# First routing of a two-pass tree network: the upper node weights loaded alone, the lower ones turned beside the token groups

## The chip, the cores and the metric

The kernel runs on one core of a Trainium2 chip. The metric is the device time of one execution in microseconds; of several executions the median is given. Engines are called as in the profile: PE (matrix products and transposes), PEld (its weight loads), DVE, ACT, POOL and SP. DMAs are issued by SP, ACT and POOL; SPq, ACTq and POOLq stand for the issuing of those queues.

## The reference, cut to what matters

```python
x = x + 0.5 * ffn(layernorm(x))        # x: (4, 1024, 256)
x = x + attention(layernorm(x))
x = x + 0.5 * ffn(layernorm(x))        # the same weights again

def fff(x, nw, nb, w1, b1, w2, b2, act):      # a tree of 255 nodes and 256 leaves
    node = 0
    for _ in range(8):
        logit = x . nw[node] + nb[node]
        node = 2 * node + 1 + (logit > 0)
    leaf = node - 255
    return act(x @ w1[leaf] + b1[leaf]) @ w2[leaf] + b2[leaf]

def ffn(x):
    xn = (x - mean) / sqrt(std + 1e-5)
    q, k, v = fff(xn, q_*), fff(xn, k_*), fff(xn, v_*)
    y = xn + softmax(q k^T / 16) v
    return y + fff(y, f_*)
```

Each of the four trees (q, k, v, f) has node weights `nw` (255 x 256), node thresholds `nb`, and for each leaf a 256x16 matrix, a 16x256 matrix and two biases.

## The kernel before, in words

The 4096 tokens are 32 tiles of 128 rows (NT = 32), taken in eight groups of four tiles (GT = 4). A tree is cut at depth 5: the 31 upper nodes decide to which of 32 blocks a token belongs, and the lower nodes are evaluated inside a block, together with the leaves. So an ffn begins with a **routing**: for each group the four tiles are normalized, turned by PE, multiplied with the upper nodes of q, k and v (`top`), compared with the thresholds (`thr`), and from the bits comes a one-hot block number `oh`; POOL adds them up in `acc`. From `oh` and `acc` the **placement** works out where each token goes (`slot`) and which token stands where (`inv`). With `inv_q` POOL gathers rows of 128 tokens of one block (`gathered`, L826), and the **leaves** of q, then k, then v run on them. Scores, softmax and the tree f follow, then the attention, then a second ffn.

What happens before the first gather is what this change touches:

- `hold_rows()` and two calls of `load_x` load the first two groups of x by SP; the other six groups are asked for inside `ffn`, behind the nodes.
- Nodes, L185 to L210. For each tree SP loads all 255 node rows in two tiles `nw` of 128 rows, PE turns them (L196), DVE copies them to `nwT` (L205), and ACT issues the load of the thresholds (L200) and the store of the lower nodes to the DRAM tensor `below` (L206). At the end the thresholds are negated (L209) and `top` is copied out of `nwT` (L210).
- L212 to L278 make small constant tables with some 45 short DVE instructions. The tables `anc` and `rights` are needed for `oh`.
- `split_b2` splits the second biases of all trees in three bfloat16 parts on POOL (casts L320, subtractions L328) and stores them in `b2i` (L323). Its loads `b_rest` are issued by ACT (L310).
- `ffn`: with `first` set, SP gets the loads of the first leaf weights (`load_raw`, 1 MB each, L718), the second leaf weights of q (`load_second`, 4 MB, named w_q<-in_q_w in the profile, L701) and the split biases (`load_b2`, L998), which wait for `b2i`.
- `routes(hp, (0, 1, 2), *hot, norms)` runs the eight groups. `norms(k)` takes means and variances of the group (L340, L341), the two square roots and reciprocals (`both_norms`, L348 to L357, and L1137), normalizes on ACT (L1165) and stores the normalized rows for the gathers (`keep_rows`, by ACT, L376). From k = 4 on it also advances `build`, which turns the leaf weights of q (L772, copies L775 and L777); the first step of `build` loads `sub` from `below` (L757) and copies it on POOL (L760).
- After `routes` come `load_b1` (48 small loads by SP, L733 and L738, with POOL work at L743 to L751) and the rest of the placement of q, whose last product is `inv_q` (L624).

The order of the instructions on each engine is not that of the program text: outside the sections marked `in_order()`, a planner places each instruction by program order and by its own estimate of when its inputs are there. On the chip each engine then runs its list strictly in order, so an instruction that waits holds everything behind it. `tc.keep_in_program_order` fixes the place of single instructions relative to others marked so.

Of the kernel before, what the change touches and what calls it, by code (L numbers as in the profile page):

```python
# [16 lines left out]
F32 = mybir.dt.float32  # L17
# [8 lines left out]
P = 128  # L26
# [4 lines left out]
KC = E // P  # L31
# [47 lines left out]
def macaron_kernel(ctx: ExitStack, tc: tile.TileContext, a: dict, out: bass.AP):  # L79
# [32 lines left out]
    def sm(shape):  # L112
        return bank("sm", shape)
# [71 lines left out]
    b2i = [dram.tile([3, B2P], BF16, name=f"b2i_{nm}") for nm in FFFS]  # L185

    with tc.tile_pool(name="nodes", bufs=2) as np_, banks(0, 8):
        nwT = np_.tile([P, KC, len(FFFS), 2 * P], F32, name="nwT", bufs=1)
        nc.vector.memset(thr, 0.0)
        for f, nm in enumerate(FFFS):  # L190
            pt = [sm([P, 2 * P]) for _ in range(KC)]
            for lo in (0, NODES - P):
                nw = np_.tile([P, E], F32, name="nw", bufs=8)
                nc.sync.dma_start(nw, a[f"{nm}_nw"][lo : lo + P, :])
                for c in range(KC):
                    nc.tensor.transpose(  # L196
                        pt[c][:, lo : lo + P], nw[:, c * P : (c + 1) * P], ident
                    )
            lo = f % 3 * NBLK
            nc.scalar.dma_start(  # L200
                thr[lo : lo + NBLK - 1, f // 3 : f // 3 + 1],
                a[f"{nm}_nb"][: NBLK - 1].unsqueeze(1),
            )
            for c in range(KC):
                nc.vector.tensor_copy(nwT[:, c, f, :NODES], pt[c][:, :NODES])  # L205
            nc.scalar.dma_start(  # L206
                below[f].rearrange("p (c n) -> p c n", c=KC), nwT[:, :, f, NBLK - 1 : NODES]
            )
        nc.vector.tensor_scalar_mul(thr, thr, -1.0)  # L209
        nc.vector.tensor_copy(top, nwT[:, :, :, :NBLK])  # L210

        nc.vector.memset(mod32, 0.0)  # L212
        t1 = np_.tile([P, 1], F32, name="t1", bufs=1)
# [86 lines left out]
    nc.vector.tensor_scalar_add(zero[:, E:], pid, float(NTOK))  # L300
    nc.gpsimd.dma_start(rows_x[NTOK:], zero[:, :E])

    def split_b2(pool):

        n = NBLK // B2G * E
        rest = pool.tile([P, n], F32, name="b2_rest")
        none = pool.tile([P, 3 * B2P // P // 2], BF16, name="b2_none")
        nc.gpsimd.memset(none, 0.0)
        for f, nm in enumerate(FFFS):
            nc.scalar.dma_start(  # L310
                rest[f * NBLK : (f + 1) * NBLK].rearrange("p (q c) -> p q c", c=E),
                a[f"{nm}_b2"].rearrange("(q p) c -> p q c", p=NBLK),
            )
            nc.gpsimd.dma_start(
                b2i[f].rearrange("s n -> (s n)").rearrange("(p i c) -> p i c", p=P, i=2),
                bc(none, 1, 2),
            )
        for s in range(3):
            part = pool.tile([P, n], BF16, name=f"b2_part{s}", tag="b2_part", bufs=2)
            nc.gpsimd.tensor_copy(part, rest)  # L320
            for f in range(len(FFFS)):
                rows = b2i[f][s].rearrange("(r n) -> r n", r=B2G)[:, : EPB * B2W]
                nc.gpsimd.dma_start(  # L323
                    rows.rearrange("r (e w) -> r e w", e=EPB)[:, :, :n],
                    part[f * NBLK : (f + 1) * NBLK],
                )
            if s < 2:
                nc.gpsimd.tensor_sub(rest, rest, part)  # L328
# [46 lines left out]
    def keep_rows(queue, lo, hi):  # L375
        queue.dma_start(  # L376
            rows_x[lo * P : hi * P].rearrange("(i p) e -> p i e", p=P), xn[:, lo:hi, :E]
        )
# [45 lines left out]
    def routes(pool, fs, oh, acc, before):  # L424


        n = NT // GT
        live = {}
        before(0)
        for k in range(n + 2):  # L430
            for j in (k - 1, k - 2, k):
                if 0 <= j < n:
                    if j == k:
                        live[k] = route(pool, fs, k * GT, oh, acc)
                    next(live[j], None)
            if k + 1 < n:
                before(k + 1)
# [551 lines left out]
    def load_b2(queue, pool, f):  # L989

        return fill_b2(
            queue, pool.tile([B2R, B2W], BF16, name=f"b2s_{FFFS[f]}", tag="b2s"), f
        )

    def fill_b2(queue, b2s, f):

        for s in range(3):
            queue.dma_start(  # L998
                b2s[s * NBLK : (s + 1) * NBLK],
                b2i[f][s, : NBLK * B2W].rearrange("(p w) -> p w", p=NBLK),  # L1000
            )
        return b2s

    def fetch(pool, f, t, slot, bufs=3, tag=None, to=None):
# [50 lines left out]
    def ffn(first: bool, last: bool):  # L1055

        def drain(*gens):
            for g in gens:
                for _ in g:
                    pass  # L1060
# [6 lines left out]
        with ExitStack() as es:  # L1067
# [31 lines left out]
            with ExitStack() as ws, banks(0, 8):  # L1099
# [8 lines left out]
                with ExitStack() as hs, ExitStack() as rs:  # L1108
# [11 lines left out]
                    with ExitStack() as rt:  # L1120
# [26 lines left out]
                            build = iter(())  # L1147
                            load_kept(nc.sync, 0, w1)
                        w2 = load_second(nc.sync, wp, 0)
                        b2s = load_b2(nc.sync, wp, 0)  # L1150
                        low, rest = placing(pq, 0, ahead=True)

                        def norms(k):
                            lo = k * GT
                            ts_ = range(lo, lo + GT)
                            if first:
                                for t in ts_:
                                    rows_moments(hp, mom[:, t, :], x_of(t))
                                both(lo, GT)
                            elif lo in (0, NT - TPB):  # L1160
                                n = TPB if lo else NT - TPB
                                both(lo, n, f"_{n}")
                            for t in ts_:
                                if first or t % 2:
                                    nc.scalar.activation(  # L1165
                                        x_of(t),
                                        x_of(t),
                                        AF.Identity,
                                        bias=shift[t],
                                        scale=scale[t],  # L1170
                                    )
                                else:
                                    nc.vector.tensor_scalar(
                                        x_of(t),
                                        x_of(t),
                                        mom[:, t, 0:1],
                                        scale[t],
                                        ALU.subtract,
                                        ALU.mult,
                                    )  # L1180
                            keep_rows(nc.scalar, lo, lo + GT)
                            if k in (4, 6):
                                drain(low(k // 2 - 2))
                            if k >= 4:
                                drain(islice(build, 2))

                        routes(hp, (0, 1, 2), *hot, norms)
                        drain(low(2))
                        if first:
                            for f in range(len(FFFS)):  # L1190
# [778 lines left out]
```

## Time and profile before

| what | value |
|---|---|
| runs | 2414.78, 2422.02, 2427.72 us; median 2422.02 us |
| the profiled execution | 2422.62 us, span 2420.8 us |
| PE busy | 2164.4 us (89%) |
| DVE, ACT, POOL busy | 1428.0 us (59%), 1073.0 us (44%), 850.1 us (35%) |
| mean granted clock of PE | 0.953 |
| from 0 to 116 us: PE, DVE, ACT, POOL busy | 57.1, 76.0, 36.5, 53.4 us |
| from 116 to 240 us: PE busy | 107.5 us |
| moved by DMA in all | 305.26 MB |

In a timeline line the first number is the start in microseconds from the start of the span, the second the time it took (or, for several merged instructions, the time they span), then engine, line, operation, the tile written and the tiles read, and the count. In brackets stands how long the engine had been idle before, and what ended that. In a line of waits the three numbers are the total, how often, and the longest one.

### The profile page before, as it was taken

What the parts mean: (1) busy time and instruction counts of PE and PEld (TensorE: products, weight loads), DVE (VectorE), ACT (ScalarE), POOL (GpSimd) and SP (SyncE); (2) the same over time, 40 slices, a digit from 0 to 9 for tenths busy, and PEclk for the clock granted to TensorE, in tenths of its full rate; (3) what the DMA queues carried; (4) which work ended last, traced back from release to release, by engine and by line L of the source; (5) the groups of instructions that cost most, each with busy time, mean ns of one, the idle gap of its engine ahead of it and who ended that gap; (6) DMA issues with size and microseconds to landing.
All of it is one profiled execution on the core that took longest, in us unless ns stands there. A gap on an engine that the chain in (4) does not pass through costs nothing. (4 is left out here: it accounts for less than half of the span.)

```text
span 2420.8 us, 43067 instructions
## 1 busy us (share of the span) xinstructions
PE 2164.4 (89%) x13969; PEld 1383.2 (57%) x13971; DVE 1428.0 (59%) x4804; ACT 1073.0 (44%) x2875; POOL 850.1 (35%) x1078
## 2 busy tenths in 40 slices
PE   4598898999997889999999999997597998999968
PEld 2377787676666744433444344334486785666657
DVE  6677655333447766666667667754775653334656
ACT  2355556233323324555555555555264663232234
POOL 4455466342524521100100110001454673245546
PEclk8799999999998979999999999999799999999989
DMA  9787776344544400000000000006568666342375
GB/s 317 243 273 227 251 227 204 103 138 122 163 146 149 150 1 1 1 1 1 1 8 12 1 3 19 17 1 228 194 187 261 170 175 206 96 140 90 125 222 170
DMA packets 201714, 305.26 MB, mean 126 GB/s; under 512 B 26185, under 2 KB 172698, under 8 KB 196864
## 3 DMA queue, kind: packets, MB, share of 16 engines
q1 hardware_dynamic: 106432, 114.60, 14.7%
q0 software_dynamic: 37264, 96.33, 14.4%
q10 hardware_dynamic: 57776, 91.32, 11.2%
q8 instruction: 125, 2.05, 0.4%
q14 instruction: 117, 0.96, 0.1%
HBM read 185.37 MB, written 121.49 MB: 127 GB/s over the span
## 5 line engine op out<-in xcount | busy, mean ns | idle before, releaser
L1719 DVE TENSOR_REDUCE mxh<-big 128x1 f32<-128x512 f32 (+3 forms) x768 | 392.7, 551 | 195.8 <-PE big L1711 194.0
L1755 ACT ACTIVATE pTh<-big 128x512 f32<-128x512 f32 (+3 forms) x768 | 341.1, 491 | 288.8 <-PE big L1711 265.0
L1711 PE MATMUL big<-kTh,qTh 32*128 32x512 f32 (+3 forms) x1536 | 403.0, 540 | 1.5 <-ACT kTh L1692 1.4
L1747 PE MATMUL big<-qTh,kTh 32*128 32x512 f32 (+3 forms) x1536 | 400.7, 537 | 1.9 <-ACT pTh L1755 1.6
L854 ACT COPY xgT<-sm 128x256 f32<-128x256 f32 x400 | 149.4, 373 | 246.1 <-PE sm L852 226.7
L1023 PE MATMUL two<-kT,qT 128*128 128x512 f32 x512 | 234.7, 602 | 10.0 <-issue 8.4
L1051 PE MATMUL sm<-vb,pT 128*128 128x256 f32 x1024 | 236.1, 384 | 0.0
L1747 PEld LDWEIGHTS big<-qTh,kTh 32*128 32x128 f32 x1536 | 143.3, 184 | 156.8 <-issue 127.0
L1051 PEld LDWEIGHTS sm<-vb,pT 128*128 128x128 f32 x1024 | 192.0, 192 | 25.6 <-issue 1.0
L852 PE MATMUL sm<-ident,xg 128*128 128x128 f32 x800 | 159.0, 281 | 37.0 <-DMA xg<-xs_f 13.0
L1031 DVE TENSOR_REDUCE mx<-two 128x1 f32<-128x1024 f32 x64 | 78.3, 1224 | 187.3 <-PE two L1023 187.3
L1766 PE MATMUL sm<-pTh,vpad 128*32 128x512 f32 (+3 forms) x1536 | 165.2, 501 | 0.0
L969 ACT COPY og<-sm 128x256 f32<-128x256 f32 x300 | 111.9, 373 | 114.8 <-DMA os_k<-og 42.4
L1711 PEld LDWEIGHTS big<-kTh,qTh 32*128 32x128 f32 x1536 | 146.6, 185 | 20.4 <-issue 14.3
L1023 PEld LDWEIGHTS two<-kT,qT 128*128 128x128 f32 x512 | 94.1, 193 | 107.3 <-issue 103.5
L893 DVE SCALAR_TENSOR_TENSOR went<-sm,sides 128x14 bf16<-128x14 f32 x400 | 67.5, 169 | 145.2 <-PE sm L884 130.1
L826 POOL DMA_INDIRECT xg<-rows_x,inv_q x100 | 102.4, 1024 | 109.5 <-PE sm L929 58.6
L826 POOL DMA_INDIRECT xg<-rows_x,inv_k x100 | 100.9, 1009 | 102.4 <-PE sm L929 70.1
L928 PE MATMUL sm<-ident,hm 128*128 128x128 f32 x400 | 110.1, 275 | 14.7 <-ACT og L969 14.7
L908 DVE TENSOR_TENSOR hm<-sm,mask 128x128 f32<-128x128 f32 x400 | 115.5, 289 | 10.5
L422 POOL TENSOR_TENSOR acc<-acc,oh 128x32 bf16<-128x32 bf16 (+1 forms) x128 | 39.8, 311 | 232.0 <-DVE oh L420 191.2
L937 ACT ACTIVATE hid<-sm 128x128 f32<-128x128 f32 x400 | 113.8, 284 | 5.9 <-PE sm L929 5.7
(373 smaller groups left out, 4424.1 us busy)
## 6 DMA issues: line engine op xcount, KB each, us to landing
xs_f<-zero ACTq DMA_DIRECT2D x14, 1028.0 KB
xg<-xs_f SPq DMA_DIRECT2D x100, 128.5 KB
os_q<-og SPq DMA_DIRECT2D x100, 128.0 KB
os_k<-og SPq DMA_DIRECT2D x100, 128.0 KB
os_v<-og SPq DMA_DIRECT2D x100, 128.0 KB
xn<-in_x SPq DMA_DIRECT2D x16, 512.0 KB
w_q<-in_q_w SPq DMA_DIRECT2D x2, 4096.0 KB
rows_x<-xn ACTq DMA_DIRECT2D x16, 512.0 KB
```

Source lines behind the costliest of these rows:

```text
L826: nc.gpsimd.indirect_dma_start(out=xg, out_offset=None, in_=rows_x, in_offset=bass.IndirectOffsetOnAxis(ap=inv[:, g : g + 1], axis=0),)
L852: nc.tensor.transpose(pa[:, c, :], xg[:, c * P : (c + 1) * P], ident)
L854: nc.scalar.copy(xT, pa)
L908: nc.vector.tensor_tensor(hm.rearrange("p (e l) -> p e l", l=LW), ph[:, :P].rearrange(split, l=LW), bc(mask[:, 0], 2, LW), ALU.mult,)
L937: nc.scalar.activation(hid, pt[:, 0], AF.Gelu if tree.f == 3 else AF.Relu)
L1023: nc.tensor.matmul(ps[:, n0 : n0 + 512], qT[:, c, i * P : (i + 1) * P], kT[:, c, n0 : n0 + 512], start=(c == 0), stop=(c == KC - 1),)
L1051: nc.tensor.matmul(po, pT[:, j, :], vb[:, j, :], start=(j == 0), stop=(j == TPB - 1))
L1711: matmul = nc.tensor.matmul(ps[:, :n], qT[r : r + HPAD, hg, i * P : (i + 1) * P], kT[r : r + HPAD, hg, n0 : n0 + n], start=True, stop=True,)
L1719: nc.vector.tensor_reduce(maxima(b, hg)[:, i, c, u : u + 1], ps[:, :n], AX.X, ALU.max)
L1747: matmul = nc.tensor.matmul(ps[:, off:], kT[r : r + HPAD, hg, j * P : (j + 1) * P], qT[r : r + HPAD, hg, qb * QN + off : (qb + 1) * QN], s ...
L1755: nc.scalar.activation(pT[:, u, off:], ps[:, off:], AF.Exp, scale=1.0 / math.sqrt(HD))
L1766: nc.tensor.matmul(acc[r : r + HPAD, off:], vpads[b % 2][:, j, 4 * hg + 2 * pair + u, :], pTs[pair][:, u, off:], start=(j == 0), stop=(j = ...
```

## The change

The nodes are no longer loaded whole before the rest. ACT loads the first 32 node rows of each tree into one tile `tops`; PE turns this tile in two transposes, and one DVE copy makes `top` for all four trees. The loads of the thresholds and of the second biases are issued by POOL instead of ACT. SP's list has no node loads between the first two loads of x and the other six.

The lower nodes are loaded, turned and stored by a new function, `keep_below`, once per tree: called from `norms(k)` for k = 1 to 4 in the first ffn. It issues two loads of 128 rows by SP into a tile with a single buffer, so that the second load waits until the first has been turned; each is turned by two transposes and copied by DVE, and the store to `below` is issued by POOL. Last, the load of the split biases of q is asked for after `routes` instead of before it, and `fill_b2` marks it to stay in program order.

```diff
     with tc.tile_pool(name="nodes", bufs=2) as np_, banks(0, 8):
-        nwT = np_.tile([P, KC, len(FFFS), 2 * P], F32, name="nwT", bufs=1)
+        tops = np_.tile([P, E], F32, name="tops", bufs=1)
         nc.vector.memset(thr, 0.0)
         for f, nm in enumerate(FFFS):
-            pt = [sm([P, 2 * P]) for _ in range(KC)]
-            for lo in (0, NODES - P):
-                nw = np_.tile([P, E], F32, name="nw", bufs=8)
-                nc.sync.dma_start(nw, a[f"{nm}_nw"][lo : lo + P, :])
-                for c in range(KC):
-                    nc.tensor.transpose(
-                        pt[c][:, lo : lo + P], nw[:, c * P : (c + 1) * P], ident
-                    )
+            nc.scalar.dma_start(tops[f * NBLK : (f + 1) * NBLK], a[f"{nm}_nw"][:NBLK, :])
+        for f, nm in enumerate(FFFS):
             lo = f % 3 * NBLK
-            nc.scalar.dma_start(
+            nc.gpsimd.dma_start(
                 thr[lo : lo + NBLK - 1, f // 3 : f // 3 + 1],
                 a[f"{nm}_nb"][: NBLK - 1].unsqueeze(1),
             )
-            for c in range(KC):
-                nc.vector.tensor_copy(nwT[:, c, f, :NODES], pt[c][:, :NODES])
-            nc.scalar.dma_start(
-                below[f].rearrange("p (c n) -> p c n", c=KC), nwT[:, :, f, NBLK - 1 : NODES]
-            )
+        pt = sm([P, KC, P])
+        for c in range(KC):
+            nc.tensor.transpose(pt[:, c, :], tops[:, c * P : (c + 1) * P], ident)
+        nc.vector.tensor_copy(top.rearrange("p c f n -> p c (f n)"), pt)
         nc.vector.tensor_scalar_mul(thr, thr, -1.0)
-        nc.vector.tensor_copy(top, nwT[:, :, :, :NBLK])
...
+    def keep_below(pool, f):
+
+        at = NBLK - 1
+        nwT = pool.tile([P, KC, NODES - at], F32, name=f"nwT_{FFFS[f]}", tag="nwT")
+        for lo in (at, NODES - P):
+            nw = pool.tile([P, E], F32, name=f"nw_{FFFS[f]}", tag="nw", bufs=1)
+            nc.sync.dma_start(nw, a[f"{FFFS[f]}_nw"][lo : lo + P, :])
+            pt = sm([P, KC, P])
+            for c in range(KC):
+                nc.tensor.transpose(pt[:, c, :], nw[:, c * P : (c + 1) * P], ident)
+            nc.vector.tensor_copy(nwT[:, :, lo - at : lo - at + P], pt)
+        nc.gpsimd.dma_start(below[f].rearrange("p (c n) -> p c n", c=KC), nwT)
...
     def split_b2(pool):
...
-            nc.scalar.dma_start(
+            nc.gpsimd.dma_start(
                 rest[f * NBLK : (f + 1) * NBLK].rearrange("p (q c) -> p q c", c=E),
...
     def fill_b2(queue, b2s, f):
         for s in range(3):
-            queue.dma_start(
+            dma = queue.dma_start(
...
+            if f == 0:
+                tc.keep_in_program_order(dma)
...
                         w2 = load_second(nc.sync, wp, 0)
-                        b2s = load_b2(nc.sync, wp, 0)
...
                             keep_rows(nc.scalar, lo, lo + GT)
+                            if first and 0 < k <= len(FFFS):
+                                keep_below(b2p, k - 1)
...
                         routes(hp, (0, 1, 2), *hot, norms)
+                        b2s = load_b2(nc.sync, wp, 0)
```

## The prediction

> **What bounds the kernel now.** The page says PE 89% busy, so I looked for where PE is not. The table of busy time by stretch shows it: from 0 to 116 us PE works 57.1 us, from 116 to 240 us 107.5 of 124, and later stretches are at 88 to 100%. The head, up to the first gather of rows (115.94 us, POOL L826; its rows reach PE at 122.47), is where PE starves, and everything behind it waits for `inv_q`. A head that ends n us sooner should therefore bring the end n us nearer. All edits lie in the head, so I read it from the timeline of each engine. ACT first:
>
> ```profile
> 6.62 0.47 ACTq L310 DMA_DIRECT2D b_rest<-in_k_b  x1
> 16.97 0.38 ACTq L310 DMA_DIRECT2D b_rest<-in_v_b  x1
> 20.30 0.59 ACTq L206 DMA_DIRECT2D below_q<-nwT  x1
> ...
> 25.04 0.32 ACTq L310 DMA_DIRECT2D b_rest<-in_f_b  x1
> 25.39 1.28 ACT L349 ACT_TABLE_LOAD   x1 [25.39 <-DVE t L274]
> ...
> 32.15 2.08 ACT L1165 ACTIVATE xn<-xn,ln_s,sd_r 128x256 f32<-128x256 f32 x4 [0.34 <-DVE ln_s L1137]
> ```
>
> ACT computes nothing for 25 us, though DVE had the first group's variances ready at 8.59 (L348: 8.44 + 0.15). The releaser named in the bracket does not matter: ACT's own list was held by DMA issues, first one that could not go out until 16.97, then the stores of the lower nodes, which need nwT. The first normalization is at 32.15. The first product with `top` (L400) is at 35.65; `top` itself was ready at 23.12.
>
> Then SP, and who waits for it:
>
> ```profile
> 30.29 0.38 SPq L701 DMA_DIRECT2D w_q<-in_q_w  x1
> 42.62 9.42 SPq L998 DMA_DIRECT2D b2s_q<-b2i_q  x2
> 52.09 0.43 SPq L757 DMA_DIRECT2D sub_q<-below_q  x1
> 52.57 0.48 SPq L733 DMA_DIRECT2D given_q<-in_q_b  x1
> 59.42 1.31 SPq L738 DMA_DIRECT2D b_q<-in_q_nb  x3
> ```
> ```profile
> SPq L738 <- DMA w_q<-in_q_w: 6.4, 1, 6.4
> ```
> ```profile
> POOL w_q L760 <- DMA sub_q<-below_q: 5.9, 1, 5.9
> ```
>
> The issue at 59.42 is the eighth on SP and ACT after w_q (rows_x twice, b2s_q, rows_x, b2s_q, sub_q, given_q between), and it waits for w_q to land: an issue goes out only when the transfer eight issues before it has landed. So the 4 MB of w_q land at 59.4, and sub_q, behind them on SP, at 62.2, where POOL stood 5.9 us for it with the sums `acc` behind (PE L551 waits 3.2 us for them).
>
> Last, DVE against POOL. POOL's two subtractions (L328, 38.39 and 47.11, 4.1 us each) lie over DVE instructions on the same group's path:
>
> ```profile
> L357 DVE TENSOR_TENSOR sd_r<-sd_r,ln_r 128x4 f32<-128x4 f32 x8 | 5.1, 632 | 0.1
> L350 DVE RECIPROCAL ln_r<-ln_r 128x4 f32<-128x4 f32 x8 | 1.3, 166 | 0.0
> ```
>
> Same four columns, 632 ns against 166: the mean holds calls of 1.28 and 2.71 us under the subtractions. From the first normalization (32.15) to the last sum (91.77) the eight groups take 59.6 us, and from there to the gather 24.2 us.
>
> **The change part by part.**
>
> *Start of the routing.* ACT's list begins with four short loads and is then free, so the first square root waits for the variances: 8.59, table load 1.28, two roots 0.4, and then as now from L350 (30.15) to the normalization (32.15) 2.0, in all 12.3. Against that, DVE has its constant tables to make, some 45 instructions from 8.84 (cst there) at about 0.15 each, 7 us, which are earlier in the program and can go first: 19.3. I take the middle, 15.8: **-16.3** (ends -19.9 and -12.9). `top` holds nothing up: two transposes (0.66 a pair at L196) and one copy (L210, 0.29) once `tops` is there, and the loads issued at 0.72 now land by 6.35.
>
> *Loads moved to POOL.* Four for thr, four for b_rest, four for below. The trace shows no plain load by POOL; its nearest rows are stores, 0.58 (L323) to 1.10 us (L314), so 7 to 13 us in all. Eight of them fall where POOL now stands idle 25.5 us (6.8 to 32.3): nothing. If that cover goes, `split_b2` begins that much later, but it now begins at 33.8 and is wanted only at 132 (L950). The four for below come among the sums, at most 4.4 us, less what POOL idles there: 0 to 4.4, I take 0, the nearest row being 0.6. The thresholds now bind until 17.89 (L209); on POOL they are wanted with the first bits, 7 us after the first normalization.
>
> The Trainium skill, "SBUF — State Buffer", section "Who interferes with whom", speaks against this move: descriptors of a GpSimd DMA are written through the port pair that DVE locks, so it advises the other queues. The rows here show little of it: the twelve L323 issues took 0.58 to 0.64 us each with DVE busy beside them. By its figure of some 3.1 us instead of 0.62 for an overlapped one, an estimate, the four stores would cost 10 us more on POOL.
>
> *x earlier.* The six loads now issued from 17.92 to 26.9 go out from about 2 us. In the trace DVE waits for x only once, 4.5 us for the first group: no gain, except that w_q follows sooner. By the stretches' rates some 19 MB had moved when w_q landed (59.4); without the lower nodes and their store (1.9 MB) and with the first 18 us at full rate, 17.1 MB: 5.0 by 18 us, the other 12.1 at the 370 GB/s of 32 to 56, w_q lands near 51.
>
> *Lower nodes beside the groups.* 16 transposes of 0.34 (L392) and 8 copies of 0.42 (L205): 5.4 us of PE, 3.3 of DVE. Between 32 and 92 PE is busy 41.2 and DVE 36.7 of 60, so most of it falls in gaps: ends 0 and 8.7, I take **+2**, nearer to the gaps. The wait it adds: the first load stands behind w_q on SP, so it lands near 51, and seven more follow one at a time, 3.4 us each (the last pair now: issued 17.07, turned 20.44). Behind the transposes in PE's list stand the groups, so where the planner puts them decides.
>
> *b2s_q after the routing.* It held SP from 30.7 to 52; SP is now held by the lower nodes instead. It is wanted at 132: nothing.
>
> Sum: 2422.62 (the profiled execution, span 2420.8) - 16.3 + 2 = 2408.3. That execution was 0.6 above the median of 2422.02, so **2408**.
>
> **The rivals.**
>
> *Deeper (0.18): 2399.* Groups then run while sub_q and given_q are not yet asked of POOL, so its waits of 5.9 and 2.7 go too. For it: DVE works only 36.7 of 60 us there. Against: sub_q is not sooner.
>
> *Given back late (0.18): 2419.* sub_q now needs w_q (51), two loads (6.8), copy and issue (1.0), store and load of 3.4 us at least: 65.6, and up to 72.4 with the 10.2 us that sub_q took. Now it lands at 62.2. If POOL's copy keeps its place among the sums, three of eight groups are held, and I price 11 of 14 us as lost. The same time results if DVE and ACT keep the first normalization behind tables and loads, near 28: then the change doesn't do what it says. The Trainium skill, "DMA: Bandwidth & Descriptors", "Rules for kernel authors", points this way: spreading DMAs over queues brings no bandwidth, all run on the same 16 engines; the row: DMA is at 1.03 to 1.09 of its share from 18 to 56. By the rule alone the head would end with its bytes, 8 us sooner.
>
> *Slower (0.12): 2436.* One mechanism, one place: PE's list has the first lower transposes behind the second group, as the program writes it, and PE stands from 20 until 51. The remaining six groups start at 51 instead of 44.71, +6.3, and of seven more round trips of 3.4 us a third is not covered, +8: about +14. It decides from the third group on: behind the fourth (53.73 now) the wait costs nothing. Against it: the planner now places loads' users near their landing (raw_q's transposes at 56.3).
>
> **How the numbers follow.** The forecast has 0.52, with own ends 2402 and 2415 from its terms. A measurement tells 0.5% from no change, 12.1 us: below 2409.9 lie the deeper case and about 0.62 of the forecast's, 0.50; above 2434.1 the slower one, 0.12; between, 0.38. The range leaves out the slower case and the far end of the deeper one: 2394 (its -23 with the start at its better end, a further -3.6) to 2428 (sub_q at 72.4, 10 us after now, with 5 us of the start kept).
>
> **What would show it.** Right: the table load before 12 us, the first normalization between 12 and 20, the last sum near 77, the first gather near 102, and PE from there as now. Wrong: a wait of PE for nw of over 10 us, POOL's wait for sub_q growing past 5.9, pitch of the groups over 7.5 us, or a gather that comes sooner while the end does not.

## The result, and the profile after

The changed kernel takes 2444.44 us, median of 9 runs (2433.83 to 2450.69), against 2423.6 for the kernel before in the same runs: ratio 1.0081, 95% interval 1.006 to 1.0102. I forecast 2408. The profiled execution took 2438.1 us, span 2436.3, which is 15.5 more than that of before. In what follows, a line of the changed kernel is 5 to 9 higher than the same line of before.

ACT's timeline shows that the first step came as forecast: the table is loaded at 2.77 us, and the first normalization, 32.15 before, is at 13.12 (forecast 15.8).

```profile
2.77 1.28 ACT L357 ACT_TABLE_LOAD   x1 [2.77 <-issue]
...
13.12 2.07 ACT L1171 ACTIVATE xn<-xn,ln_s,sd_r 128x256 f32<-128x256 f32 x4 [1.35 <-DVE ln_s L1144]
```

PE's timeline shows where it ends. The column after the start is the busy time; the bracket tells the idle time before it and its releaser.

```profile
13.78 2.16 PE L397 MATMUL sm<-ident,xn 128*128 128x128 f32 x8
51.52 0.69 PE L304 MATMUL sm<-ident,nw_q 128*128 128x128 f32 x2 [35.58 <-DMA nw_q<-in_q_nw]
55.36 0.69 PE L304 MATMUL sm<-ident,nw_q 128*128 128x128 f32 x2 [3.15 <-DMA nw_q<-in_q_nw]
55.84 3.11 PE L405 MATMUL sm<-xT,top 128*96 128x512 f32 x4
...
63.63 0.41 PE L304 MATMUL sm<-ident,nw_k 128*128 128x128 f32 x2 [3.59 <-DMA nw_k<-in_k_nw]
63.87 1.88 PE L405 MATMUL sm<-xT,top 128*96 128x512 f32 x4
```

PE turns the first group's tiles until 15.9 and then stands 35.58 us for nw_q: the transposes of the lower nodes (L304) stand in its list ahead of the *first* group's product with `top` (L405), which comes at 55.84 instead of 35.65. From there each group carries a pair of loads and lasts 7 to 8 us. SP's timeline shows why nw_q is late; here the second column is how long the issue itself took:

```profile
22.12 0.48 SPq L706 DMA_DIRECT2D w_q<-in_q_w  x1
25.41 18.21 SPq L301 DMA_DIRECT2D nw_q<-in_q_nw  x1
43.67 0.63 SPq L738 DMA_DIRECT2D given_q<-in_q_b  x1
44.34 7.59 SPq L743 DMA_DIRECT2D b_q<-in_q_nb  x3
...
52.53 0.53 SPq L301 DMA_DIRECT2D nw_q<-in_q_nw  x1
...
60.46 0.43 SPq L762 DMA_DIRECT2D sub_q<-below_q  x1
```

```profile
SPq L743 <- DMA w_q<-in_q_w: 6.4, 1, 6.4
```

w_q is asked for at 22.12. The issue of nw_q right behind it takes 18.21 us, until 43.6, and its rows land at 51.5. The second of the three merged issues of b_q waits 6.4 us for w_q, from 44.76 on, so w_q landed near 51.2, as forecast (near 51). The second half of nw_q can only be asked for when the first has left its one buffer (52.53).

POOL's longest wait up to 135 us (us in total, times, longest) and three lines of its timeline tell the rest:

```profile
POOL below_q L306 <- DVE ln_r L355: 26.2, 1, 26.2
```

```profile
56.81 0.62 POOL L306 DMA_DIRECT2D below_q<-nwT_q  x1 [26.20 <-DVE ln_r L355]
...
105.06 3.46 POOL L427 TENSOR_TENSOR acc<-acc,oh 128x96 bf16<-128x96 bf16 x8 [0.56 <-DVE oh L425]
...
132.14 1.04 POOL L831 DMA_INDIRECT xg<-rows_x,inv_q  x1 [19.41 <-issue]
```

The first store of lower nodes holds POOL 26.2 us, with the rest of the splits behind it; the DVE row named does not matter: what the store needs is nwT_q, whose second half DVE copies at 56.08, once PE has turned nw_q. The 5.9 us wait for sub_q is gone, since sub_q lands before POOL comes to it. The last sum ends at 108.5 (91.77 before), the first gather is at 132.14 (115.94 before): 16.2 later, and the end 15.5. Of the two DVE rows shown before, the product (L362 here) is back at 158 ns; POOL's first subtraction, at 26.54, now lies over another row, of which one call took 4.41 us (from 26.23):

```profile
L353 DVE TENSOR_SCALAR ln_r<-mom 128x4 f32<-128x4 f32 x8 | 5.5, 693 | 0.0
...
L355 DVE RECIPROCAL ln_r<-ln_r 128x4 f32<-128x4 f32 x8 | 1.2, 166 | 0.0
L362 DVE TENSOR_TENSOR sd_r<-sd_r,ln_r 128x4 f32<-128x4 f32 x8 | 1.2, 158 | 0.1
```

**All runs.** Times of the profile: first normalization, last sum, first gather, first gather of the *second* network's rows (which shows how far the leaves are). The ratio is to the kernel before on the same chip, medians of 6 to 12 runs against 9 to 35. The edits are told in the next section. A star: runs in which the kernel before takes 2512 to 2520 us, instead of 2421 to 2424. Times of starred and other runs are therefore compared with care: three pairs that do not differ up to the second network's rows (e13 and e21, e14 and e23, e16 and e22) are 0.3 to 1.3 us later at the first gather in the starred run, and 1.3 to 2.0 at the second rows.

| kernel | norm | sum | gather | 2nd rows | ratio (95%) |
|---|---|---|---|---|---|
| before | 32.15 | 91.8 | 115.9 | 208.6 | 1 |
| changed | 13.12 | 108.5 | 132.1 | 225.8 | 1.0081 (1.006-1.0102) |
| e1* | 13.06 | 96.1 | 121.2 | 217.3 | 1.0038 (1.0017-1.0059) |
| e3* | 12.96 | 99.0 | 128.8 | 234.8 | 1.0095 (1.0068-1.0122) |
| e6* | 13.08 | 96.2 | 124.2 | 222.4 | 1.005 (1.0024-1.0076) |
| e4* | 16.84 | 95.4 | 120.2 | 217.6 | 1.0024 (1.0003-1.0044) |
| e7 | 31.67 | 87.2 | 111.1 | 204.4 | 0.9982 (0.996-1.0004) |
| e8 | 16.64 | 84.3 | 110.2 | 214.4 | 1.0019 (1.0-1.0039) |
| e9 | 16.70 | 83.4 | 109.1 | 208.3 | 0.9998 (0.9981-1.0015) |
| e10 | 16.68 | 86.5 | 114.1 | 210.8 | 1.0037 (1.0022-1.0052) |
| e13 | 16.68 | 82.1 | 108.3 | 201.0 | 1.0036 (1.0021-1.0051) |
| e14 | 12.73 | 83.4 | 109.0 | 201.7 | 1.0038 (1.0022-1.0054) |
| e15 | 31.14 | 91.8 | 115.7 | 208.8 | 1.008 (1.0056-1.0105) |
| e16 | 31.45 | 87.8 | 112.1 | 204.3 | 1.0061 (1.0038-1.0085) |
| e17 | 16.66 | 81.6 | 107.0 | 210.3 | 1.0031 (1.0016-1.0047) |
| e18 | 12.73 | 85.5 | 110.5 | 221.6 | 1.0074 (1.0051-1.0096) |
| e20 | 31.43 | 96.9 | 122.7 | 215.7 | 1.0018 (1.0001-1.0035) |
| e21* | 15.39 | 82.7 | 108.6 | 202.2 | 0.9979 (0.996-0.9999) |
| e22* | 31.59 | 89.5 | 113.4 | 206.3 | 0.9991 (0.9968-1.0013) |
| e23* | 12.61 | 83.9 | 110.2 | 203.0 | 0.9973 (0.9955-0.9992) |

### The profile page after: what moved, and what is told of

It reads as the page before. It is cut to its first block, busy times and chain, and to the rows that moved or that the text cites. A ratio compares the mean times of both kernels' runs of the same rounds, so it can differ in the third digit from the quotient of the medians.

```text
span 2436.3 us, 43076 instructions
## 1 busy us (share of the span) xinstructions
PE 2152.5 (88%) x13973; PEld 1378.5 (57%) x13973; DVE 1427.2 (59%) x4804; ACT 1072.7 (44%) x2875; POOL 856.4 (35%) x1090
## 3 DMA queue, kind: packets, MB, share of 16 engines
q1 hardware_dynamic: 106432, 114.60, 14.5%
q10 hardware_dynamic: 55664, 89.49, 10.9%
## 5 line engine op out<-in xcount | busy, mean ns | idle before, releaser
L1030 PEld LDWEIGHTS two<-kT,qT 128*128 128x128 f32 x512 | 94.6, 194 | 108.3 <-issue 104.5
L831 POOL DMA_INDIRECT xg<-rows_x,inv_q x100 | 102.5, 1025 | 114.1 <-PE sm L934 56.5
L933 PE MATMUL sm<-ident,hm 128*128 128x128 f32 x400 | 110.2, 276 | 14.2 <-ACT og L974 14.2
L913 DVE TENSOR_TENSOR hm<-sm,mask 128x128 f32<-128x128 f32 x400 | 115.6, 289 | 10.5
```

What stands on the lines that cost most here:

```text
L831: nc.gpsimd.indirect_dma_start(out=xg, out_offset=None, in_=rows_x, in_offset=bass.IndirectOffsetOnAxis(ap=inv[:, g : g + 1], axis=0),)
L913: nc.vector.tensor_tensor(hm.rearrange("p (e l) -> p e l", l=LW), ph[:, :P].rearrange(split, l=LW), bc(mask[:, 0], 2, LW), ALU.mult,)
L1030: nc.tensor.matmul(ps[:, n0 : n0 + 512], qT[:, c, i * P : (i + 1) * P], kT[:, c, n0 : n0 + 512], start=(c == 0), stop=(c == KC - 1),)
```

## The experiments

### Is it PE's wait behind w_q? (e1, e3, e6)

Theory W: PE stands for lower nodes that come late because they stand behind w_q on SP. Rival D: the DMA engines are full, and the lower nodes would be as late from any place in any line.

e1: the changed kernel, the lower nodes asked for behind x and turned there, ahead of all groups, with eight buffers for nw instead of one and four for nwT.

```diff
         nc.vector.tensor_scalar_mul(thr, thr, -1.0)
+        for lo in range(2 * GT, NT, GT):
+            load_x(lo)
+        for f in range(len(FFFS)):
+            keep_below(np_, f)
...
-                            if first and 0 < k <= len(FFFS):
-                                keep_below(b2p, k - 1)
```

> The changed kernel with the lower nodes asked for right behind the eight loads of x, ahead of raw_q and w_q, into eight buffers of the nodes' own pool, and turned there; all else as changed. Theory W (PE stands in front of the lower nodes because their load lies behind the 4 MB of w_q on SP): PE's wait of 35.6 us falls under 12 us, first gather near 103 to 110 us instead of 132, time 2408 to 2416 us. Rival D (the 16 DMA engines are full, the place in SP's list does not matter): the first lower nodes land after 35 us all the same, time above 2430. Rival P (POOL, which now issues the stores of the lower nodes, holds the sums): the stores still stand in POOL's list, so less than half comes back, above 2430.

e3: w_q asked for behind the routing.

```diff
-                        w2 = load_second(nc.sync, wp, 0)
...
                         routes(hp, (0, 1, 2), *hot, norms)
+                        w2 = load_second(nc.sync, wp, 0)
                         b2s = load_b2(nc.sync, wp, 0)
```

> The changed kernel with only the load of w_q moved behind the routing; PE's order is unchanged. W: the first lower nodes stand behind x and raw_q only (6.3 MB instead of 10.5), land near 25 to 30 us instead of 51.5, time 2415 to 2428 us against 2444. D: with the engines as full, they land after 40, time above 2436.

e6: the lower nodes asked for by ACT.

```diff
-            nc.sync.dma_start(nw, a[f"{FFFS[f]}_nw"][lo : lo + P, :])
+            nc.scalar.dma_start(nw, a[f"{FFFS[f]}_nw"][lo : lo + P, :])
```

> The changed kernel with the eight loads of the lower nodes issued by ACT instead of SP, nothing else moved. W: out of SP's line they land within 10 us of their issue near 15 us, PE's wait falls from 35.6 to under 12, time 2412 to 2428 us. D: they land after 40 us on any queue, time 2440 or more.

PE's first product in e1, e3 and e6 is at 29.67, 37.96 and 26.40 instead of 55.84. In e3's PE timeline the first wait is 18.08 us; in e6's it is 9.66, but 7.93 and 5.83 follow:

```profile
33.85 0.69 PE L304 MATMUL sm<-ident,nw_q 128*128 128x128 f32 x2 [18.08 <-DMA nw_q<-in_q_nw]
37.48 0.69 PE L304 MATMUL sm<-ident,nw_q 128*128 128x128 f32 x2 [2.94 <-DMA nw_q<-in_q_nw]
37.96 3.62 PE L405 MATMUL sm<-xT,top 128*96 128x512 f32 x4
...
47.45 0.66 PE L304 MATMUL sm<-ident,nw_k 128*128 128x128 f32 x2 [4.05 <-DMA nw_k<-in_k_nw]
47.90 3.62 PE L405 MATMUL sm<-xT,top 128*96 128x512 f32 x4
```

```profile
25.92 0.69 PE L304 MATMUL sm<-ident,nw_q 128*128 128x128 f32 x2 [9.66 <-DMA nw_q<-in_q_nw]
...
38.73 0.69 PE L304 MATMUL sm<-ident,nw_k 128*128 128x128 f32 x2 [7.93 <-DMA nw_k<-in_k_nw]
45.24 0.66 PE L304 MATMUL sm<-ident,nw_k 128*128 128x128 f32 x2 [5.83 <-DMA nw_k<-in_k_nw]
```

W holds for the first wait and D falls: with the place in line changed, both halves of nw_q are turned 17.9 (e3) and 29.4 us (e6) sooner. In e6 no byte is taken away, and the DMA engines are as full as in the changed kernel: 1.05 against 1.01 of their share from 14 to 52 us. In e3 the next trees' lower nodes come 10 us apart, one buffer and one round trip after the other, so the gather is only 3.3 us sooner than in the changed kernel. Behind it the late w_q costs more than that: from 125 to 240 us PE waits 19.1 us for gathered rows, in four waits, instead of 5.8 in one. The ratio is 1.0095, as slow as the changed kernel. With the lower nodes out of w_q's line, in their own buffers and ahead of the groups (e1) the loss is halved, 1.0038; which of these three edits does it was not taken apart. But no kernel of the three is faster than before, though e1's PE waits only 13.1 us for nw_q and has its first product 6.0 us sooner than before (29.67 against 35.65). W alone does not explain that; it opened the second question.

The Trainium skill says in "DMA: Bandwidth & Descriptors", "Rules for kernel authors", that spreading DMAs over queues brings no bandwidth. e6 agrees as far as bytes go (361 GB/s from 14 to 52 us, 349 in the changed kernel) and shows what the rule leaves out: a place in another line brings the same rows 29.4 us sooner (25.92 instead of 55.36).

### Where does an early routing go? (e4, e7 to e10)

e4: the kernel before, in which only the issues of thr, of the second biases and of the lower nodes' stores move to POOL. The three edits, twelve issues in all, are of one kind, of which the first is shown. The lower nodes are turned on PE ahead of the groups, as before; the first normalization is at 16.84, and the first product with `top` at 20.34.

```diff
-            nc.scalar.dma_start(
+            nc.gpsimd.dma_start(
                 thr[lo : lo + NBLK - 1, f // 3 : f // 3 + 1],
```

> The kernel before with one part of the change alone: thresholds, second biases and the stores of the lower nodes issued by POOL instead of ACT; nodes loaded and turned where they were. W: this part is the good one, ACT is free, the first normalization comes at 13 to 20 us instead of 32, the first product with top follows top at 24 to 27 instead of 35.65, time 2410 to 2418 us. P: POOL's issues cost more than they free, time 2424 or above.

The head is no nearer its end: the sums end at 95.4, the gather is at 120.2. POOL's timeline names the place:

```profile
58.75 0.30 POOL L760 COPY w_q<-sub_q 128x64 f32<-128x64 f32 x1 [12.42 <-DMA sub_q<-below_q]
```

POOL stands 12.42 us for sub_q, with the splits already behind it and the sums interleaved with the biases' work after it. sub_q lies behind w_q on SP, as before: its issue there takes 17.11 us (20.18 in e1, 0.33 in e7, where w_q is not ahead). So routing that starts 15 us sooner arrives at sums that wait for w_q. Four kernels take this apart.

e7: the kernel before, w_q and b2s_q behind the routing. e8: e4 with the same. e9: e4 with the sums by VectorE. e10: both. The first cut is e7's, the second e9's.

```diff
-                        w2 = load_second(nc.sync, wp, 0)
-                        b2s = load_b2(nc.sync, wp, 0)
...
                         routes(hp, (0, 1, 2), *hot, norms)
+                        w2 = load_second(nc.sync, wp, 0)
+                        b2s = load_b2(nc.sync, wp, 0)
```
```diff
-            nc.gpsimd.tensor_tensor(acc[:, i + 1], acc[:, i], oh[:, i], ALU.add)
+            nc.vector.tensor_tensor(acc[:, i + 1], acc[:, i], oh[:, i], ALU.add)
```

> The kernel before, with one edit: the 4 MB of w_q and its three loads of b2s are asked for behind the routing instead of ahead of it. Theory P (the 4 MB in SP's line make sub_q, and the biases behind it, late, and with them GpSimd's list, in which the running sums stand): sub_q lands before 45 us instead of 62.2, GpSimd's wait of 5.9 us for it is gone, its last sum ends some 3 to 6 us sooner than the 91.8 of before, the first gather by as much, and the time is 0 to 0.25% below before. Theory S (the groups themselves set the head's end: the start of the routing at 32 us and 60 us of groups): the sums end within 2 us of before, ratio 1.000 within its error. A loss of over 0.3% would say that w_q, asked for late, is wanted before it has landed.

> The kernel before with the four loads of thr, the four of the second biases and the four stores of the lower nodes issued by GpSimd (which brought the first normalization to 16.8 us and the head no nearer), and in addition w_q and b2s_q asked for behind the routing. Theory P: sub_q lands before 45 us, the waits of 12.4 us for it and 3 to 4 us for the given biases go from GpSimd's list, the sums end near 80 to 85 instead of 95, the first gather comes near 105 to 110, and the time is 0.3 to 0.6% below before. Theory S2 (the early groups meet the split of the second biases on GpSimd, which is 24 us of work wherever it stands): the sums end within 4 us of 95 and the time is within 0.3% of before, on the slow side.

> The same twelve issues by GpSimd, w_q where it was, and the 32 running sums of the routing added by VectorE instead of GpSimd, so that nothing on the routing's path stands in GpSimd's list any more. If GpSimd's list is what took the early start back (P and S2 alike), the last sum follows the last bits by a few us, near 82, the first gather comes near 106, and the time is 0.3 to 0.6% below before. If it is not (the sums end past 92 here too), the groups are held by DVE or PE, which the rows then show, and the time stays within 0.3% of before or above it.

> Both: twelve issues by GpSimd, w_q and b2s_q behind the routing, sums by VectorE. If GpSimd's list alone held the head, this is equal to the kernel with the sums by VectorE and w_q ahead (within 0.15%). If w_q's 4 MB also slow the routing by what they take of the DMA engines, it is the faster of the two by 0.1 to 0.3%; if w_q is wanted before it has landed behind the first gather, it is the slower.

Theory P holds for the sums: they end at 84.3 in e8 and 83.4 in e9 instead of 95.4, and the gather is at 110.2 and 109.1, 6 to 7 us sooner than before. It fails for the time: 1.0019 and 0.9998. In e10 POOL stood 33.0 us for given_f, which its text does not have, and the gather came at 114.1; that is still sooner than before, so this wait alone does not give its 1.0037. Only e7, with nothing of the change, lies more than 0.1% below before, and its interval holds 1. A gather that comes sooner no longer brings the end nearer. ACT's timeline of e9 shows what is late next:

```profile
108.92 1.31 ACTq L701 DMA_DIRECT2D w_k<-in_k_w  x1
118.72 0.37 ACT L854 COPY xgT<-sm 128x256 f32<-128x256 f32 x1 [12.33 <-PE sm L458]
119.50 0.37 ACT L854 COPY xgT<-sm 128x256 f32<-128x256 f32 x1 [0.40 <-PE sm L852]
119.56 7.78 ACTq L757 DMA_DIRECT2D sub_v<-below_v  x1
127.38 0.37 ACT L854 COPY xgT<-sm 128x256 f32<-128x256 f32 x1 [7.51 <-issue]
```

```profile
114.13 0.44 ACTq L701 DMA_DIRECT2D w_k<-in_k_w  x1
...
124.57 0.37 ACT L854 COPY xgT<-sm 128x256 f32<-128x256 f32 x1 [1.03 <-PE sm L852]
124.63 1.00 ACTq L757 DMA_DIRECT2D sub_v<-below_v  x1
127.23 0.37 ACT L854 COPY xgT<-sm 128x256 f32<-128x256 f32 x1 [2.29 <-PE sm L852]
```

The gathered rows reach PE at 118.0, 4.4 us sooner than before, and ACT copies two of them (`xgT`). Then it has to issue sub_v, behind the 4 MB of w_k in its own line, and that takes 7.78 us (10.89 in e8, 1.00 before). The place behind w_k is not enough for it, since before sub_v is asked for as soon after w_k (10.5 us, 10.6 in e9); in e9 the clears of the next section still compete with w_k. The third copy is at 127.38 in e9 and 127.23 before: all of the gain is gone. The DMA engines are at 1.05 of their share from 100 to 130 us, and at 0.53 from 60 to 100 (columns at the end: granted clock of PE, DMA share, GB/s):

```profile
60.00:100.00 40.00, 24.02 (x112) 15.39 (x112) 31.53 (x84) 11.73 (x24) 21.43 (x39) 0.67 0.53 157
100.00:130.00 30.00, 10.10 (x50) 7.82 (x48) 13.60 (x62) 2.99 (x8) 13.83 (x21) 0.56 1.05 351
```

### What fills the DMA engines there? (e13 to e20)

Of the bytes moved there, 5.1 MB are three clears of output rows (os_q, os_k, os_v, 1664 KB each), on SP from 93 us on. e13: e9 with the clears behind the first network's leaves. e14: the same edit and sums by VectorE on e1. e15: the kernel before with this edit alone. e16: e7 with it.

```diff
-                    if first:
-                        for f in range(3):
-                            tc.keep_in_program_order(clear(nc.sync, osrt[f][SPARE[1] * P :]))
...
                         with_steps(islice(main, steps), (1, islice(places, steps)), *sides)
+                        if first and not f:
+                            for g in range(3):
+                                tc.keep_in_program_order(clear(nc.sync, osrt[g][SPARE[1] * P :]))
```

> The kernel before with the twelve issues by GpSimd and the running sums by VectorE (first gather at 109.1 us, 6.8 sooner than before, but the time the same), and in addition the three clears of the output rows' tails (1664 KB each, issued on SP at 94 us before) asked for behind the first network's leaves. Theory F (behind the first gather the full DMA engines take the gain back: the rows land late, and ACT stands 7.8 us for the issue of sub_v, which waits for a transfer eight issues older, in the middle of the leaves' first copies): with 5.1 MB less in the way, DMA is below 0.8 of its share from 105 to 115, the wait of ACT for that issue is under 2 us, the leaves run at full pace from about 118 instead of 130, and the time is 0.3 to 0.6% below before. Rival C (PE's granted clock, 0.50 to 0.67 there until PE has been busy for a while, or the leaves' own pace takes it back): the wait goes and the time stays within 0.2% of before.

> The changed kernel with its three costs taken away: the lower nodes asked for by SP right behind x and turned there (no longer behind w_q), the running sums by VectorE, and the clears behind the first network's leaves. If the change's idea, the early upper nodes, is sound and only these three places took it back, it is 0.4 to 0.8% below before and equal to or up to 0.2% below the kernel before with the same two edits and the twelve issues by GpSimd. If the early upper nodes bring nothing that the twelve moved issues do not bring, the two are within 0.15% of each other.

> The kernel before with the three clears alone moved behind the first network's leaves. Theory F: the gather stays at 116 us, since nothing ahead of it changes, but the rows of the first gathers land sooner: PE's 5.1 us wait for them is about 2.5 us, and the leaves start 2 to 5 us sooner; the time is 0.1 to 0.25% below before. If the clears cost nothing where they are, the time is within 0.1% of before; if they collide with the writes of the leaves' outputs or the loads of the next network, it is 0.1 to 0.3% above.

> The kernel before with w_q and b2s_q behind the routing (gather at 111.1, time 0.18% below before) and the clears behind the first network's leaves, so nothing of the change in it. It tells whether the early routing is needed for a gain at all: theory F with a sound early routing has this at 0.2 to 0.4% below before, and the two kernels with the early routing 0.15% or more below this one; if the early start of the routing is worth nothing, this is as fast as they are, or faster.

All four are slower than before, which theory F did not have (e15's text names it as possible, at a third of the size), and all for one reason. Up to 215 us e13 does what theory F says: sub_v's issue takes 0.40 us, DMA is at 0.35 of its share from 100 to 110, and the second network's rows are asked for at 201.0, 7.7 us sooner. So rival C does not take the start back. Nor does sub_v wait for an older transfer, as e13's text has it: in e9 the profile puts ACT's 7.51 us to "issue", and in e13, with w_k 10.9 us ahead in the same line but no clears beside it, the same issue is short. Then PE stands 21.1 us (21.7, 21.6 and 20.2 in the others), because the leaves' outputs on SP stand behind the clears. ACT's issue in e13, PE's longest wait there from 200 to 260 us, and SP:

```profile
117.32 0.40 ACTq L757 DMA_DIRECT2D sub_v<-below_v  x1
```

```profile
PE sm L928 <- ACT og L969: 21.1, 1, 21.1
```

```profile
200.41 17.98 SPq L970 DMA_DIRECT2D os_q<-og  x11
218.49 0.39 SPq L332 DMA_DIRECT2D os_q<-zero  x1
...
221.09 8.42 SPq L332 DMA_DIRECT2D os_v<-zero  x1
229.61 31.20 SPq L970 DMA_DIRECT2D os_k<-og  x10
```

In e15 the gather stays where it was (115.7), and the leaves start no sooner for the clears being away (208.8): in the kernel before, the clears cost the leaves' start nothing. e14 and e13 are 0.02% apart, so the early upper nodes bring nothing here that the twelve moved issues do not bring.

e17: e9 with the clears issued by POOL, among the splits of the biases. e18: the same on e1 with sums by VectorE. e20: the kernel before with sums by VectorE and the clears by POOL behind the splits.

```diff
                         routes(hp, (0, 1, 2), *hot, norms)
+                        if first:
+                            for f in range(3):
+                                tc.keep_in_program_order(clear(nc.gpsimd, osrt[f][SPARE[1] * P :]))
```

> The kernel before with the twelve issues by GpSimd, the sums by VectorE, and the three clears issued by GpSimd among the second and third split of the second biases (about 48 to 60 us) instead of by SP at 94. With the clears behind the first network's leaves the leaves began 7.7 us sooner than before, but PE then stood 21.6 us near 230, behind ACT and SP, for the clears themselves. Theory F (after the gather it is the bytes still to be moved that hold the leaves' start): the clears fill the time from 60 to 100 us in which DMA is at 0.24 to 0.8 of its share; the leaves start as early (first gather of the second network's rows near 201), no 21 us wait follows, and the time is 0.3 to 0.6% below before. Rival L (the early 5.1 MB hold up the small loads of the biases and GpSimd's list with them): the first gather is later than 109, and the time is within 0.2% of before or above it.

> The changed kernel with the lower nodes asked for right behind x and turned there, the sums by VectorE, and the clears by GpSimd among the splits. If the idea of the change is sound and only the three places named took it back, it is 0.3 to 0.7% below before and within 0.2% of the kernel that only moved the twelve issues and has the same two edits. If it is at or above before, the early start of the routing is lost somewhere that these edits do not touch.

> The kernel before with the sums by VectorE and the clears by GpSimd behind its third split (about 62 us), and nothing of the change: the control for the other two. If the early start is worth what it shows at the last sum (83 instead of 92), this one is 0.2 to 0.4% slower than they are. If it is as fast as they are, the gain is the two edits' and the early start of the routing brings nothing.

Rival L was right in its cause, not in its place: the biases' small loads come late behind 5.1 MB. POOL waits 14.5 us for given_v in e17, 15.0 in e18, 18.6 for b_k in e20. In e17 the first gather is early (107.0), but in e17 and e18 POOL's list has biases' work between the first gathers, and the second network's rows are asked for at 210.3 and 221.6. The control e20, with nothing of the change, is not slower than they are (1.0018 against 1.0031 and 1.0074), so no gain of the early routing shows in these three.

### Does a sooner start of the leaves reach the end? (e21 to e23)

The clears in 39 pieces of 128 KB, one beside each leaf of the second network from its 16th on. e21: on e9. e22: on e7. e23: on e1 with sums by VectorE, that is, the change itself with the costs found so far taken out.

```diff
+                        def cleared():
+                            for _ in range(15):
+                                yield
+                            for g in range(3):
+                                for lo in range(SPARE[1] * P, NSLOT, P):
+                                    tc.keep_in_program_order(clear(nc.sync, osrt[g][lo : lo + P, :]))
+                                    yield
+                        if first and f:
+                            sides += ((1, cleared()),)
```

> The kernel before with the twelve issues by GpSimd, the sums by VectorE, and the three clears cut into 39 pieces of 128 KB, issued by SP one beside each leaf of the second network from its 16th on, when w_v has landed. Theory F: with the clears out of the head the first gather of the second network's rows comes near 201 us instead of 208.6, and as each piece is no larger than a leaf's own output, no wait of over 4 us follows on PE; the end keeps the 7 to 8 us: 0.25 to 0.4% below before. Rival G (something between 210 and 830 us, DMA for the next weights above all, takes it back whatever the leaves' start): the second network's rows are asked for near 201, a wait grows elsewhere, and the time is within 0.15% of before or above it.

> The kernel before with w_q and b2s_q behind the routing and the clears in the same 39 pieces: nothing of the early routing. First gather near 111 to 112, the second network's rows near 204 (4 us before the kernel before), the time 0.1 to 0.25% below before; by theory F it is 0.1 to 0.15% slower than the kernel with the early routing and the same pieces.

> The changed kernel with the lower nodes asked for behind x and turned there, the sums by VectorE, and the clears in the 39 pieces. Its rows of the second network were asked for near 202 us with the clears out of the head. By theory F 0.2 to 0.4% below before, so some 1.1% below the changed kernel as it stands; by rival G within 0.15% of before or above it.

e21 is at 0.9979 (0.996 to 0.9999) and e23 at 0.9973 (0.9955 to 0.9992): the two versions that beat both kernels, e21 barely. The expected sizes were 0.25 to 0.4 and 0.2 to 0.4%, so e21 came out just below its range. The two are 0.06% apart: again the upper nodes alone bring nothing beyond the moved issues. No 21 us wait follows: PE's longest for these outputs from 200 to 300 us in e23 is 3.6. Whether the early routing is needed for it is not settled: e22, without it, is at 0.9991, and the intervals overlap.

## Why the prediction was wrong

**Start of the routing: right.** 13.12 against 15.8, table load before 12, `top` no hindrance.

**Loads moved to POOL: right as costs, blind to a wait.** The twelve issues took 0.53 to 0.77 us each in the changed kernel, the four stores of lower nodes 0.58 to 0.62. So of the 3.1 us that the Trainium skill gives in "SBUF — State Buffer", "A bandwidth-pool intuition that's wrong (but worth ruling out)", for an issue beside a DVE copy, nothing shows; no DVE instruction beside them lasted over 0.75 us. What shows is a stretch between computations: the DVE call of 4.41 us beside POOL's subtraction takes 0.16 otherwise. Of the two calls that I put under the subtractions before, only the one of 2.71 us lies there; the one of 1.28, at 43.19, lies under a cast of POOL (42.54 to 44.46). But I priced the stores as issues only. The first of them waits for nwT and held POOL 26.2 us. What that alone costs was not tried; sums could not have run meanwhile, since PE stood too.

**x earlier: right.** No gain of its own, w_q landed near 51.2.

**b2s_q: no wait for it shows.** The leaves' product with it does not wait for DMA.

**Lower nodes beside the groups, +2: this step failed.** I took the load to land near 51, which is what it did. But the +2 is the work of PE and DVE alone; the wait for the load I put at nothing in the sum, because I supposed the transposes behind later groups or near their landing. I gave the right mechanism 0.12, put it behind the second group, and priced it at 14. It was behind the *first* group's transposes, and it decided from the first group on: PE stood 38.7 us for nw_q alone, the first product with `top` came 20.2 us later than before, and the gather came 30 us after the 102 I had named. With the loads out of w_q's line and turned ahead of the groups (e1) the gather is 11.0 sooner (121.2), and the loss is 0.38% instead of 0.81%.

**"A head that ends n us sooner should bring the end n us nearer": this failed too, and it carried the forecast.** The step counted from the first normalization to the end. e4 has the whole of it without any lower nodes between the groups on PE, 15.3 us sooner at the normalization, and is 0.24% slower. Of the 15 us, POOL's list behind sub_q takes all in e4; with the sums out of it (e9) 8.3 are left at the last sum and 6.8 at the gather; at ACT's third copy, 0. I had written that everything behind the head waits for `inv_q`; from the moment that `inv_q` is early, it waits for the transfers that still run there, w_k and the clears, instead: with the clears away (e13) the second network's rows come 7.7 us sooner.

What comes nearest to following the end is the pace of the leaves, read from the first gather of the second network's rows. Against before it moved by +17.2 (changed), -4.2 (e7), +5.8 (e8), -0.3 (e9), +7.1 (e20) and +13.0 us (e18); the ratios times 2423 give +19.6, -4.4, +4.6, -0.5, +4.4 and +17.9. The moves are those of one execution each; e8's is the slowest of its twelve (2439.5, median 2426.8). In the starred runs, from e21 to e3 it is 32.6 us in the one and 1.16%, 29 us, in the other. e13 to e16 stand outside, by 16 to 19 us, near the 20 to 21.7 that PE later stands for their clears. e10 and e17 are 6 to 7 us slower than this reading. By the first gather of the third network's rows, 313.6 before, e17 is 7.0 us late (320.6) and e10 4.6 (318.2), so all of it in e17 and half in e10 comes up among the second network's leaves; I found no single wait that explains it, and it stays open. This is a reading over many kernels; no run moves the start of the leaves alone.

**The rivals.** "Slower" at 2436 was the case, with the profiled execution at 2438.1, but that its number is so near is partly luck: it has the groups 6.3 us later and 8 us of round trips, and in the run the first product is 20.2 us later, while from there to the last sum the groups take 52.7 us instead of 56.1. "Given back late" names sub_q behind w_q; in the changed kernel POOL does not wait for sub_q, but in e4 that wait is what takes the start back. I had it as an alternative to "slower" instead of beside it.

## What to carry to other kernels

When work is moved to an earlier place, follow its gain to the engine that does the last step, and ask at each list (here POOL's for sub_q, then ACT's for sub_v) what it meets there; the gain ends at the first list that is not early too. A load that feeds PE must not stand behind megabytes in its line, and its transposes must not stand in PE's list ahead of work that is ready. Choose as the milestone the first point that the rest follows: here the first gather of the second network came far nearer to that than the first gather of the first.

## What the runs showed of the hardware

In four runs an issue right behind the 4 MB of w_q in the same line stayed in its engine until shortly before w_q landed. The issue behind w_q was done at 51.5 (before), 43.6 (changed), 50.0 (e4) and 46.0 (e6); w_q's landing, read from the wait for it in a later issue, was at 59.4, near 51.2, 57.9 and 52.8: 6.8 to 7.9 us later in each. On SP that holds up loads, on ACT computation: 7.78 us between two copies in e9, where the landing of w_k is not known. Without the 4 MB ahead the same issues took 0.33 (sub_q in e7) and 0.50 us (nw_q in e3). How long such an issue is held depends on what else moves: behind w_k, 10.5 to 10.9 us after it, sub_v's issue took 1.00 us before, 7.78 in e9 and 0.40 in e13.

TensorE's granted clock was 0.52 (before) and 0.56 (e9) of full from 100 to 130 us, where PE is busy 44 and 34% of the time, and 1.00 from 132 on in both. The slow clock lies over the wait for rows there; what it adds was not measured.
